# A 17-tap convolution by transforms of 48 tokens instead of 32, in groups of 16 graphs

## The chip, the core and the metric

The kernel runs on one core of a Trainium2 chip. A core has several engines that run side by side, each through its own list of instructions in order: TensorE (PE; its weight loads are listed as PEld) multiplies matrices into a memory of its own, PSUM; VectorE (DVE) and ScalarE (ACT) compute on PSUM and on the on-chip memory SBUF; GpSimd (POOL) computes on SBUF alone; SyncE (SP) issues transfers. Transfers between DRAM and SBUF can be issued by SyncE, ScalarE and GpSimd and are carried out by 16 DMA engines. The engines wait for each other through semaphores.

The metric is the time of one execution on the device, in microseconds (us). The kernel before took 2396.99 us (median of three runs, 2395.56 to 2398.62).

## What is computed

64 graphs of 256 tokens with 256 features, all in fp32, go through two layers. Layer 0 is a normalized graph convolution with a residual and a layer norm. Layer 1 takes its result `x` through two ways into a gated unit:

```python
xc = jnp.transpose(x, (0, 2, 1))
h = relu(bn1(conv1d(xc, conv1_w, 0)))            # 1 tap
h = bn2(conv1d(h, conv2_w, 8))                   # 17 taps, 256 -> 256 channels
x_conv = jnp.transpose(relu(h + xc), (0, 2, 1))
s = x @ w_se.T + b_se                            # 3 features
A = exp(-dist(s)) * adj
x_nmp = A @ relu(x @ w_msg.T + b_msg)
x_in = concat([x_conv, x_nmp], -1)
gi, gh = x_in @ w_ih.T + b_ih, x @ w_hh.T + b_hh # 3 * 256 outputs each
r, z = sigmoid(gi_r + gh_r), sigmoid(gi_z + gh_z)
y = (1 - z) * tanh(gi_n + r * gh_n) + z * x
out = layernorm(x + y)
```

The change concerns the second convolution, `conv2`, and the ways of data around it.

## The kernel before

`conv2` is done by the overlap-save method along the tokens. A window of `FL` = 32 tokens gives `NT` = 16 new outputs, because 17 taps need 16 more inputs. Each window is transformed to frequencies (a matmul with a fixed table), each frequency is multiplied by the transformed taps (a 256 x 256 matrix per frequency, again matmuls), and the inverse transform is done by additions and scaled additions on VectorE. A graph has `GT` = 256 / 16 = 16 windows, so that `Q` = 8 graphs fill the 128 partitions; there are `NQ` = 8 such groups.

The forward transform of a graph, a part of `layer1`:

```python
for k in range(DCH):                              # two halves of the channels
    p = bank("p_dft")
    for c, t0, t1 in ((0, 0, mid + 1), (1, mid - 1, GT)):
        first = t0 + 1 - c * mid
        nc.tensor.matmul(p[:, t0 * FL : t1 * FL], h[:, c, k * P : (k + 1) * P],
                         fwd[:, first : first + t1 - t0, :].rearrange("p t f -> p (t f)"), ...)
    nc.scalar.copy(V[:, :, k, g % Q * GT : (g % Q + 1) * GT], p.rearrange("p (t f) -> p f t", f=FL))
```

The products, two frequencies to a step. A complex frequency takes three real products, with `V` real, `V` imaginary and their sum `ab`; the taps `u` were transformed in a setup stage, stored in DRAM, and are loaded for each group again:

```python
def product(p, j, v, u):
    for k in range(DCH):
        nc.tensor.matmul(p[:, j * D : (j + 1) * D], v[:, k, :], u[:, k, :], start=k == 0, stop=k == DCH - 1)
# in products(), for each step:
for t, v in ((0, ab), (1, V[:, n0:n1]), (2, V[:, NF + n0 : NF + n1])):
    p = accbank(f"p_k{t}")
    for j in range(count):
        product(p, j, v[:, j], load_u(3 * (n0 + j) + t))
    p = half(p)[:, :count]
    if t == 0:   nc.scalar.copy(re, p)
    elif t == 1: nc.vector.tensor_add(im, re, p)
    else:        nc.vector.tensor_sub(re, re, p)
    yield
```

`FREQ` has 15 complex frequencies, and there are two real ones. The results go to a buffer `M` of their own. The inverse transform works in place in `M` (`even_frequencies`, `odd_frequencies`); the residual is added into `M` by a DMA that accumulates, issued by GpSimd; then `outputs` transposes `M` on TensorE and writes `xcT`, the gate's input with channels on the partitions, for the whole group:

```python
def residual(q, M):
    for i in range(4):
        nc.gpsimd.dma_start(M[:, i:16:4, :], xt[:, :, i % 2, i // 2, :], accum_op=ALU.add)
```

The gate of a graph, in two halves `c` of 128 tokens. Each half has two pieces on TensorE, `p_rz` and `p_n`:

```python
q = accbank("p_rz")                               # 6 matmuls of 512 columns
for j, (lhsT, w) in enumerate(hid + inp):
    nc.tensor.matmul(q, lhsT, w[:, : 2 * D], ...)
yield
p = accbank("p_n")                                # 6 matmuls of 256 columns
...
nc.vector.tensor_add(trz[:, c, :], q, brz_t)
nc.scalar.activation(trz[:, c, :], trz[:, c, :], AF.Tanh, scale=0.5)
...                                               # gn on VectorE, nn on ScalarE
# once per graph:
nc.gpsimd.tensor_tensor(total, x1, nn, op=ALU.add)
nc.gpsimd.tensor_tensor(x1, x1, nn, op=ALU.subtract)
...
layernorm(x1, nc.vector)
nc.sync.dma_start(out[g].rearrange("(c p) d -> p c d", p=P), x1)
```

Layer 0 and layer 1 of a graph leave `x1` (for the residual and the gate) and `xn` (for the gate) in DRAM; both stores are issued by GpSimd.

The stages are recorded piece by piece, so that pieces of several stages alternate in each engine's list; a scheduler may move instructions within it. A group's products alternate with gates of the group before, the inverse transform with further gates, and the graphs of the next group with the remaining pieces:

```python
for step in range(STEPS):                         # products of group q
    if step < 4: run(products(V, M, step))
    else:        run(merge(products(V, M, step), take(even, 2)))
    run(take(late, (0, 1, 1, 1, 2, 2, 2, 1)[step]))   # gates of the group before
run(even)
residual(q, M)
...                                               # late, odd and the first layer-0 pieces alternate
run(graphs(first, V, others))                     # layer 0 and 1 of the next 8 graphs, with early gates
```

Of the kernel before, what the change touches and what calls it, by code (L numbers as in the profile page):

```python
# [14 lines left out]
P = 128  # L15
# [11 lines left out]
def kernel(  # L27
# [36 lines left out]
    FL, NT = 32, 16  # L64
# [3 lines left out]
    assert N == 256 and D == 256 and B % Q == 0 and TAPS == FL - NT + 1  # L68
# [37 lines left out]
    make_identity(nc, ident)  # L106
    neg_half = const.tile([P, 4], F32)
# [61 lines left out]
    FREQ = (-8, 4, -12, 2, 10, -14, -6, 1, 5, 9, 13, -15, -11, -7, -3)  # L169
    NF = len(FREQ)  # L170
    NU = 3 * NF + 2
    SETS = (24, NU - 24)
    GC = 4
    GW = D // GC
    KT = GC * TAPS

    fm_rows = 2 * P + NT
    fm = dram.tile([fm_rows, FL], F32, name="fm")
    ud = [dram.tile([s * GC, GW, D], F32, name=f"ud{i}") for i, s in enumerate(SETS)]
    fwd = const.tile([P, GT // 2 + 2, FL], F32)  # L180
    dft_w = const.tile([KT, NU, GC], F32)

    def tables(pool):
        period = pool.tile([1, 512], F32, name="period")
# [3 lines left out]
        def wave(f, sine, n):  # L188

            first = 0 if not sine else (24 if f > 0 else 8)  # L190
            return period[:, first : first + abs(f) * (n - 1) + 1 : abs(f)]

        fwd_row = pool.tile([1, FL, FL], F32, name="fwd_row")
        w_row = pool.tile([1, TAPS, NU], F32, name="w_row")
        for n, f in enumerate(FREQ):
            nc.vector.tensor_copy(fwd_row[:, :, n], wave(f, False, FL))
            nc.vector.tensor_copy(fwd_row[:, :, NF + n], wave(-f, True, FL))

            c, d = wave(f, False, TAPS), wave(f, True, TAPS)
            nc.vector.tensor_copy(w_row[:, :, 3 * n], c)  # L200
            nc.vector.tensor_sub(w_row[:, :, 3 * n + 1], d, c)
            nc.vector.tensor_add(w_row[:, :, 3 * n + 2], c, d)
        for r in range(2):
            nc.vector.memset(fwd_row[:, :, 2 * NF + r], 1.0)
            nc.vector.memset(w_row[:, :, 3 * NF + r], 0.5)
        nc.vector.memset(fwd_row[:, 1::2, 2 * NF + 1], -1.0)
        nc.vector.memset(w_row[:, 1::2, 3 * NF + 1], -0.5)
# [5 lines left out]
        nc.gpsimd.dma_start(fm[P - 8 : P - 8 + FL].unsqueeze(0), fwd_row)  # L213
        for j in range(GT // 2 + 2):

            first = P - 8 + 8 - NT * (j - 1)
            nc.sync.dma_start(fwd[:, j, :], fm[first : first + P])


        wd = dram.tile([TAPS, NU], F32, name="wd")  # L220
        nc.gpsimd.dma_start(wd.unsqueeze(0), w_row)
        wt = pool.tile([KT, NU], F32, name="wt")
        for c in range(GC):
            nc.sync.dma_start(wt[c * NT : (c + 1) * NT], wd[:NT])
        nc.sync.dma_start(wt[GC * NT :], bcast_rows(wd[NT], NU, GC))
        mask = pool.tile([KT, GC], F32, name="mask")
        nc.vector.tensor_reduce(
            mask[: GC * NT], ident[: GC * NT, : GC * NT].rearrange("p (c t) -> p c t", c=GC), AX.X, ALU.add
        )
        nc.vector.tensor_copy(mask[GC * NT :], ident[GC * NT : KT, GC * NT : KT])  # L230
        nc.vector.tensor_mul(
            dft_w, wt.unsqueeze(2).to_broadcast([KT, NU, GC]), mask.unsqueeze(1).to_broadcast([KT, NU, GC])
        )

    def weights(pool, n, parts, scale):
# [5 lines left out]
        for c in range(GC):  # L241
            nc.sync.dma_start(tp[c * NT : (c + 1) * NT], taps[c, :NT])
        nc.sync.dma_start(tp[GC * NT :], taps[:, NT])
        nc.vector.tensor_mul(tp, tp, scale[:KT].unsqueeze(1).to_broadcast([KT, ng, D]))
        first = 0
        for i, count in enumerate(SETS):
            m = count * GC
            u = pool.tile([m, ng, D], F32, name=f"u_set{i}")
            for j in range(0, ng, 2):
                p = accbank("p_u").rearrange("p (g o) -> p g o", g=2)  # L250
                for h in range(2):
                    nc.tensor.matmul(  # L252
                        p[:m, h], dft_w[:, first : first + count, :].rearrange("p s c -> p (s c)"), tp[:, j + h],
                        start=True, stop=True,
                    )
                nc.scalar.copy(u[:, j : j + 2], p[:m])
            nc.gpsimd.dma_start(ud[i][:, n * ng : (n + 1) * ng], u)
            first += count
            yield
# [24 lines left out]

    x1_d = [dram.tile([Q, N, D], F32, name=f"x1_d{q}") for q in range(NQ)]
# [4 lines left out]
    def layer0(g):  # L290
# [5 lines left out]
        nc.vector.tensor_reduce(deg, a_t, AX.X, ALU.add)  # L296
# [51 lines left out]
        nc.gpsimd.dma_start(x1_d[g // Q][g % Q].rearrange("(c p) d -> p c d", p=P), x1)  # L348
        yield

    def layer1(g, V):

# [56 lines left out]
# [4 lines that stand above are left out]
# [7 lines left out]
                V[:, :, k, g % Q * GT : (g % Q + 1) * GT], p.rearrange("p (t f) -> p f t", f=FL)  # L420
# [20 lines left out]
        nc.gpsimd.dma_start(xn_d[g], xn)  # L441
# [4 lines left out]
    RE = (1, 4, 6, 8, 9, 10, 11) + tuple(range(16, 24))  # L446
    IM = (3, 5, 7, 12, 13, 14, 15) + tuple(range(24, 32))

    def load_u(slot):
        i, s = (0, slot) if slot < SETS[0] else (1, slot - SETS[0])  # L450
        u = ustream.tile([P, DCH, D], F32, name="u")
        nc.sync.dma_start(
            u, ud[i][s * GC : (s + 1) * GC].rearrange("c g o -> (c g) o").rearrange("(k p) o -> p k o", p=P)
        )
        return u
# [9 lines left out]
    def frequencies(step):  # L465
        return (0, 1) if step == 0 else (2 * step - 1, 2 * step + 1)

    AB = {}

    def sums(V, step):  # L470
        n0, n1 = frequencies(step)
        AB[step] = freq.tile([P, 2, DCH, P], F32, name="ab", bufs=2)
        nc.vector.tensor_add(AB[step][:, : n1 - n0], V[:, n0:n1], V[:, NF + n0 : NF + n1])

    def products(V, M, step):

        n0, n1 = frequencies(step)
        count = n1 - n0
        ab = AB.pop(step)
        if step + 1 < STEPS:  # L480
            sums(V, step + 1)
        if step == 0:
            p = accbank("p_real")
            for r in range(2):
                product(p, r, V[:, 2 * NF + r], load_u(3 * NF + r))
# [5 lines left out]
        def slots(of):  # L491
            by = of[n1 - 1] - of[n0] if count == 2 else 1
            return M[:, of[n0] : of[n0] + (count - 1) * by + 1 : by, :]

        re, im = slots(RE), slots(IM)
        for t, v in ((0, ab), (1, V[:, n0:n1]), (2, V[:, NF + n0 : NF + n1])):
            p = accbank(f"p_k{t}")
            for j in range(count):
                product(p, j, v[:, j], load_u(3 * (n0 + j) + t))
            p = half(p)[:, :count]  # L500
            if t == 0:
                nc.scalar.copy(re, p)
            elif t == 1:
                nc.vector.tensor_add(im, re, p)
            else:
                nc.vector.tensor_sub(re, re, p)
# [12 lines left out]
    def four(M, re, im):  # L519


        def parts(first, count):
            return bass.AP(
                tensor=M.tensor, offset=M.offset + first * D,
                ap=[list(M.ap[0]), [(im - re) * D, 2], [1, count * D]],
            )
        sub2(parts(re, 2), parts(re + 2, 2))
        sub2(parts(re, 1), parts(re + 1, 1))
# [3 lines left out]
    def turn(x, y, num, den):  # L532

        t = freq.tile([P, 2, D], F32, name="turn", bufs=2)
        a = math.pi * num / den
        stt = nc.vector.scalar_tensor_tensor
        if 2 * num <= den:
            tan = math.tan(a)
            stt(t[:, 0, :], y, -tan, x, op0=ALU.mult, op1=ALU.add)
            stt(t[:, 1, :], x, -tan, y, op0=ALU.mult, op1=ALU.subtract)  # L540
            return math.cos(a), t
        cot = 1.0 / math.tan(a)
        stt(t[:, 0, :], x, cot, y, op0=ALU.mult, op1=ALU.subtract)
        stt(t[:, 1, :], y, -cot, x, op0=ALU.mult, op1=ALU.subtract)
        return math.sin(a), t
# [4 lines left out]
    def even_frequencies(M):  # L550

        stt = nc.vector.scalar_tensor_tensor
# [12 lines left out]
        four(M, 8, 12)  # L565
# [3 lines left out]
        for i, num, x, y in ((1, 2, 9, 13), (2, 1, 10, 14), (3, 3, 15, 11)):  # L569
            by, t = turn(M[:, x, :], M[:, y, :], num, 8)  # L570
            stt(M[:, 8 + i : 16 : 4, :], t, -by, M[:, i:8:4, :], op0=ALU.mult, op1=ALU.add)
# [4 lines left out]
    def residual(q, M):  # L576

        xt = x1_d[q].rearrange("g (t a b c) d -> (g t) a b c d", t=GT, b=2, c=2)
        for i in range(4):
            nc.gpsimd.dma_start(M[:, i:16:4, :], xt[:, :, i % 2, i // 2, :], accum_op=ALU.add)  # L580

    def odd_frequencies(M):

        stt = nc.vector.scalar_tensor_tensor
        def parts(first, count, by=8):
            return bass.AP(
                tensor=M.tensor, offset=M.offset + first * D, ap=[list(M.ap[0]), [by * D, 2], [1, count * D]]
            )
        sub2(parts(16, 4), parts(20, 4))
        yield  # L590
        four(M, 16, 24)
        yield
        r = math.sqrt(0.5)
        add2(M[:, 20, :], M[:, 30, :])
        sub2(M[:, 28, :], M[:, 22, :])
        sub2(parts(21, 1), parts(23, 1))
# [267 lines left out]
```

## Time and profile before

| what | value |
|---|---|
| time, median of 3 | 2396.99 us |
| span of the profiled execution | 2394.0 us |
| busy: TensorE / VectorE / ScalarE / GpSimd | 2258.0 / 1422.7 / 712.9 / 546.0 us |
| DMA | 289.71 MB, mean 121 GB/s |
| loads of transformed taps (`u`) | 376 of 256 KB |
| granted TensorE clock, mean | 0.986 |

How to read the profile: "L460" is line 460 of the kernel. A group of instructions has its engine, its operation, the tile that it writes and those that it reads, the shape and the count. One fp32 matmul of the kernel appears as two records on PE; a transpose appears as one. In the table of stages each row is a stretch of the span with the busy time of each engine in it, the share of full speed at which TensorE's clock ran, and the share of the DMA engines' time with their GB/s. In the 40 slices a digit is a busy share in tenths.

### The profile page before, as it was taken

Reading aid. Unit: us, or ns where it says so; the run is one execution under the profiler, and the core shown is the slowest. Engines: PE = TensorE matmul, PEld = TensorE weight load, DVE = VectorE, ACT = ScalarE, POOL = GpSimd, SP = SyncE. Lnnn points to the kernel's source line nnn. Section 1 sums busy time; section 2 is a strip of 40 time slices with the busy share of each in tenths; the row PEclk is TensorE's granted clock in tenths of the full one; section 3 lists DMA queues with packets and bytes.
Section 4 is the critical chain, followed back from the end, with each engine's and each line's share of the span. In section 5 each row is a group of like instructions: output and inputs, shape, how many; then the busy total and the mean of one; then the engine's idle time right before and its main releaser. Section 6 shows DMA issues by size and latency. Waiting matters only on the chain.

```text
span 2394.0 us, 26937 instructions
## 1 busy us (share of the span) xinstructions
PE 2258.0 (94%) x9056; PEld 1604.4 (67%) x9056; DVE 1422.7 (59%) x3740; ACT 712.9 (30%) x1417; POOL 546.0 (23%) x587
## 2 busy tenths in 40 slices
PE   5999899999999999999999989999999999999997
PEld 4777666766777677766767666676677667776554
DVE  4445854776456845567456665477645684456644
ACT  2553253114331143212431134311433124321111
POOL 3220222213221222112220222221222122211122
PEclk8999999999999999999999999999999999999999
DMA  5777622743237322472225622274223732146121
GB/s 113 202 190 250 162 78 67 199 140 92 76 114 197 111 75 88 134 197 80 79 88 163 168 79 93 66 200 140 91 80 113 196 110 75 67 133 166 56 67 44
DMA packets 226018, 289.71 MB, mean 121 GB/s; under 512 B 19208, under 2 KB 202760, under 8 KB 224377
## 3 DMA queue, kind: packets, MB, share of 16 engines
q1 hardware_dynamic: 189112, 207.19, 29.3%
q0 software_dynamic: 33360, 79.88, 11.9%
q8 instruction: 72, 1.18, 0.2%
q10 hardware_dynamic: 3408, 0.93, 0.2%
q14 instruction: 66, 0.53, 0.1%
HBM read 208.46 MB, written 79.47 MB: 120 GB/s over the span
## 4 chain that ended last, share of the span: by engine, by line
PE 36%; issue 33%; POOL 12%; DVE 11%; DMA 5%; ACT 3%; SPq 0%; POOLq 0%; ACTq 0%; DVEq 0%
PE p_k L460 7%; PE p_rz L664 6%; PE p_n L669 5%; PE p_nmp L436 3%; PE p_dft L414 3%; POOL ln_rs L270 3%; DMA u<-ud 3%; POOL x_g L692 3%; POOL total L691 3%; PE p_u L252 2%; PE p_msg L392 2%; PE p_hT L330 2%; PE p_out L340 2%; DVE ln_st L267 1%; PE p_conv L368 1%
## 5 line engine op out<-in xcount | busy, mean ns | idle before, releaser
L664 PE MATMUL p_rz<-whh,xn_g 128*128 128x512 f32 x512 | 247.6, 600 | 0.0
L664 PE MATMUL p_rz<-wih,xcT 128*128 128x512 f32 x512 | 242.5, 594 | 4.8 <-ACT xcT L629 4.8
L664 PE MATMUL p_rz<-wih,xn_g 128*128 128x512 f32 x512 | 241.1, 593 | 0.0
L691 POOL TENSOR_TENSOR total<-x_g,nn 128x512 f32<-128x512 f32 x64 | 97.3, 1520 | 615.8 <-ACT nn L683 574.2
L460 PE MATMUL p_k<-u,V 128*128 128x256 f32 x960 | 222.7, 382 | 8.0 <-DMA u<-ud 7.0
L683 ACT ACTIVATE nn<-gn 128x256 f32<-128x256 f32 x128 | 53.3, 417 | 572.3 <-DVE gn L680 572.3
L460 PEld LDWEIGHTS p_k<-u,V 128*128 128x128 f32 x960 | 179.7, 190 | 41.7 <-issue 8.6
L674 ACT ACTIVATE trz<-trz 128x512 f32<-128x512 f32 x128 | 80.4, 628 | 416.8 <-DVE trz L673 297.6
L664 PEld LDWEIGHTS p_rz<-wih,xcT 128*128 128x128 f32 x512 | 96.5, 190 | 127.8 <-issue 117.5
L664 PEld LDWEIGHTS p_rz<-wih,xn_g 128*128 128x128 f32 x512 | 97.2, 191 | 120.4 <-issue 120.4
L673 DVE TENSOR_TENSOR trz<-p_rz,brz_t 128x512 f32<-128x512 f32 x128 | 87.2, 681 | 111.2 <-PE p_rz L664 111.2
L676 DVE TENSOR_TENSOR gn<-p_n,bn_t 128x512 f32<-128x512 f32 x128 | 88.1, 688 | 106.6 <-PE p_n L669 106.4
L270 POOL TENSOR_TENSOR ln_rs<-ln_rs,neg_half 128x2 f32<-128x2 f32 x128 | 95.9, 750 | 237.7 <-DVE ln_rs L269 164.2
L414 PE MATMUL p_dft<-fwd,h 128*128 128x288 f32 x512 | 140.2, 413 | 8.3 <-ACT h L373 3.6
L340 PE MATMUL p_out<-w,hT 128*128 128x256 f32 x512 | 129.0, 397 | 19.6 <-ACT hT L335 19.6
L392 PE MATMUL p_msg<-wmsg,xn 128*128 128x256 f32 x512 | 123.9, 385 | 21.4 <-DVE s L371 11.1
L280 ACT ACTIVATE x<-x,ln_mr,ln_rs 128x256 f32<-128x256 f32 x128 | 70.0, 593 | 242.5 <-DVE ln_mr L278 242.5
L669 PE MATMUL p_n<-whh,xn_g 128*128 128x256 f32 x512 | 138.4, 391 | 0.0
L431 DVE TENSOR_TENSOR aT<-aT,adjT 128x512 f32<-128x512 f32 x64 | 44.2, 691 | 154.0 <-ACT aT L430 154.0
L669 PE MATMUL p_n<-wih,xcT 128*128 128x256 f32 x512 | 133.3, 380 | 0.0
L664 PEld LDWEIGHTS p_rz<-whh,xn_g 128*128 128x128 f32 x512 | 94.3, 193 | 56.9 <-issue 51.7
L669 PE MATMUL p_n<-wih,xn_g 128*128 128x256 f32 x512 | 132.3, 381 | 0.0
(139 smaller groups left out, 4197.6 us busy)
## 6 DMA issues: line engine op xcount, KB each, us to landing
u<-ud SPq DMA_DIRECT2D x376, 256.0 KB, 3.8
xn_d<-xn POOLq DMA_DIRECT2D x64, 512.0 KB, 3.2
xn_g<-xn_d SPq DMA_DIRECT2D x64, 512.0 KB, 3.7
adj_t<-in_adj_dram SPq DMA_DIRECT2D x64, 256.0 KB, 3.0
x_t<-in_x_dram SPq DMA_DIRECT2D x64, 256.0 KB, 2.9
x_d<-x POOLq DMA_DIRECT2D x64, 256.0 KB, 3.2
x_g<-x_d SPq DMA_DIRECT2D x64, 256.0 KB, 2.7
M<-x_d POOLq DMA_DIRECT2D x32, 512.0 KB, 12.0
```

What stands on the lines that cost most here:

```text
L270: nc.gpsimd.tensor_tensor(rs, rs, neg_half[:, :NCH], op=ALU.pow)
L340: nc.tensor.matmul(p[:, c, :], hT[:, k, c * P : (c + 1) * P], w0[:, k, :], start=k == 0, stop=k == DCH - 1)
L392: nc.tensor.matmul(p[:, c, :], x1T[:, k, c * P : (c + 1) * P], wmsg[:, k, :], start=k == 0, stop=k == DCH - 1)
L414: nc.tensor.matmul(p[:, t0 * FL : t1 * FL], h[:, c, k * P : (k + 1) * P], fwd[:, first : first + t1 - t0, :].rearrange("p t f -> p (t f)") ...
L436: nc.tensor.matmul(p[:, k, :], msg[:, mc, k * P : (k + 1) * P], aT[:, mc].rearrange("p n q -> p (n q)"), start=mc == 0, stop=mc == NCH - 1,)
L460: nc.tensor.matmul(p[:, j * D : (j + 1) * D], v[:, k, :], u[:, k, :], start=k == 0, stop=k == DCH - 1)
L664: nc.tensor.matmul(q, lhsT, w[:, : 2 * D], start=j == 0, stop=j == len(terms) - 1)
L669: nc.tensor.matmul(p[:, o * D : (o + 1) * D], lhsT, w[:, 2 * D :], start=j == 0, stop=j == len(terms) - 1)
L673: nc.vector.tensor_add(trz[:, c, :], q, brz_t)
L674: nc.scalar.activation(trz[:, c, :], trz[:, c, :], AF.Tanh, scale=0.5)
L676: nc.vector.tensor_add(gn, p.rearrange("p (i d) -> p i d", i=2), bn_t)
L691: nc.gpsimd.tensor_tensor(total, x1, nn, op=ALU.add)
```

## The change

The window becomes `FL` = 48 tokens with `NT` = 32 new outputs, so that a graph has 8 windows and a group 16 graphs; there are 4 groups. A larger window spends a smaller part of its products on the 16 tokens that overlap. What goes with it:

- The products are written in place of their inputs: `V` and `M` are one buffer, `VM`. A second, half-size buffer `V2` takes the inputs of the first 8 graphs of the next group meanwhile, and ScalarE copies them over later.
- The taps are transformed with the real and the imaginary part; their sum and difference are made by GpSimd and VectorE. The setup stage covers 16 graphs.
- The inverse transform is rewritten (`real_transform`, `complex_begin` during the products, `complex_end` after them). Its outputs go to DRAM with tokens as rows (`xc_d`); each gate loads its graph's rows back, adds the residual by an accumulating DMA, and transposes them.
- The stores of `x1`, `xn` and `out` are issued by ScalarE; the degree sums and the last norm's scaling are done by ScalarE.

```diff
-    FL, NT = 32, 16
+    FL, NT = 48, 32
...
-    FREQ = (-8, 4, -12, 2, 10, -14, -6, 1, 5, 9, 13, -15, -11, -7, -3)
+    FREQ = tuple(3 * k for k in (-4, 2, -6, 1, 5, -7, -3)) + tuple(3 * k + 1 for k in (*range(8), *range(-8, 0)))
...
-        nc.vector.tensor_reduce(deg, a_t, AX.X, ALU.add)
+        for c in range(NCH):
+            nc.scalar.activation(unused, a_t[:, c, :], AF.Copy, accum_out=deg[:, c : c + 1])
...
-        nc.gpsimd.dma_start(x1_d[g // Q][g % Q].rearrange("(c p) d -> p c d", p=P), x1)
+        nc.scalar.dma_start(x1_d[g // Q][g % Q].rearrange("(c p) d -> p c d", p=P), x1)
...
-        nc.gpsimd.dma_start(xn_d[g], xn)
+        nc.scalar.dma_start(xn_d[g], xn)
...
+    VM = freq.tile([P, FL, D], F32, name="VM")
+    V, M = VM.rearrange("p f (k q) -> p f k q", k=DCH), VM
...
+        for t, v in ((1, of_pair(V, RE, step)), (0, ab), (2, of_pair(V, IM, step))):
+            q = accbank(f"p_k{t}")
+            for j, n in enumerate(PAIRS[step]):
+                product(q, j, v[:, j], load_u(n, t))
+            p[t] = half(q)[:, :count]
+            if t == 0:
+                nc.scalar.copy(re, p[0])
+            elif t == 2:
+                nc.vector.tensor_add(im, re, p[1])
+                nc.vector.tensor_sub(re, re, p[2])
+            yield
...
+    def output(q, n, re, im):
+        plain = M[:, n // 8 * 8 + ORDER.index(n % 8), :]
...
+        for j in range(2):
+            stt(M[:, low + 16 * j, :], t[:, j, :], by[j], plain, op0=ALU.mult, op1=ALU.add)
+        nc.gpsimd.dma_start(
+            xc_d[q].rearrange("g (t a b) d -> (g t) a b d", a=2, b=16)[:, :, n, :], M[:, low : low + 17 : 16, :]
+        )
...
+        xc = gate.tile([P, NCH, D], F32, name="xc_g")
+        nc.sync.dma_start(xc, xc_d[g // Q][g % Q].rearrange("(c p) d -> p c d", p=P))
...
+    def residual(g):
+        nc.gpsimd.dma_start(
+            GATE[g][2], x1_d[g // Q][g % Q].rearrange("(c p) d -> p c d", p=P), accum_op=ALU.add
+        )
...
+    def transposed(g):
+        x1, xn, xc = GATE[g]
+        xcT = gate.tile([P, DCH, N], F32, name="xcT")
+        p = bank("p_xcT").rearrange("p (k n) -> p k n", k=DCH)
         for k in range(DCH):
+            for c in range(NCH):
+                nc.tensor.transpose(p[:, k, c * P : (c + 1) * P], xc[:, c, k * P : (k + 1) * P], ident)
+            nc.scalar.activation(xcT[:, k], p[:, k], AF.Relu, bias=bn2[:, 1, k : k + 1])
+        GATE[g] = x1, xn, xcT
...
-        layernorm(x1, nc.vector)
-        nc.sync.dma_start(out[g].rearrange("(c p) d -> p c d", p=P), x1)
+                layernorm(x1, nc.scalar)
+                nc.scalar.dma_start(out[g].rearrange("(c p) d -> p c d", p=P), x1)
...
+    AHEAD = Q // 2
+    V2 = ahead.tile([P, FL, DCH, AHEAD * GT], F32, name="V2")
...
             else:
-                run(merge(products(V, M, step), take(even, 2)))
-            run(take(late, (0, 1, 1, 1, 2, 2, 2, 1)[step]))
-        run(even)
-        residual(q, M)
+                run(merge(products(step), take(real, 1)))
+                run(complex_begin(step))
+            if q:
+                run(take(late, (0, 1, 1, 1, 1, 1, 2, 1, 2, 1, 2, 1)[step]))
+            else:
+                run(take(begin, 2 + step // 4))
+        run(real)
+        if not q:
+            run(merge(begin, end, 3))
+        elif more:
+            run(merge(merge(take(late, 18), take(begin, 6), 3), take(end, 8), 3))
+            run(begin)
+        else:
+            run(merge(late, end, 2))
         if more:
...
+            run(late)
+            run(end)
+            for f in range(0, FL, 12):
+                nc.scalar.copy(V[:, f : f + 12, :, : AHEAD * GT], V2[:, f : f + 12])
+            early = gates(q, range(EARLY))
+            others = [take(early, 2) for _ in range(Q)]
+            run(graphs(first, range(AHEAD, Q), V, others))
+            run(early)
+            late = gates(q, range(EARLY, Q))
         else:
-            run(outputs(M, xcT))
-            run(gates(q, range(Q), xcT))
+            run(gates(q, range(Q)))
```

## The prediction

> **What bounds the kernel now.** I read the busy shares first, then two stretches of TensorE's timeline for its pace, then the busy table of chosen stages, then the groups that the change touches.
>
> The page's busy shares and slices:
>
> ```profile
> PE 2258.0 (94%) x9056; PEld 1604.4 (67%) x9056; DVE 1422.7 (59%) x3740; ACT 712.9 (30%) x1417; POOL 546.0 (23%) x587
> PE   5999899999999999999999989999999999999997
> ```
>
> TensorE is busy nearly everywhere; no other engine exceeds 59%. Busy time alone does not say how near TensorE is to its rate, because matmuls overlap. The timeline of TensorE in the last gate stage does (start, busy, group):
>
> ```profile
> 2280.81 1.88 PE L664 MATMUL p_rz<-whh,xn_g 128*128 128x512 f32 x4
> 2282.53 1.88 PE L664 MATMUL p_rz<-wih,xn_g 128*128 128x512 f32 x4
> 2284.25 1.88 PE L664 MATMUL p_rz<-wih,xcT 128*128 128x512 f32 x4
> 2285.96 1.03 PE L669 MATMUL p_n<-whh,xn_g 128*128 128x256 f32 x4
> ```
>
> Four records of 512 columns start 1.72 us apart: 430 ns each. Four of 256 columns, in the same timeline, take 0.865 us: 216 ns each. So 0.84 ns a column, against listed durations of 600 and 382 ns. I use these paces (also 242 ns for 288 columns, 109 ns for 128).
>
> At these paces the work of TensorE is: 1536 records of 512 columns, 660 us; 5856 of about 256 (1536 p_n, 1504 p_k and p_real, 2560 in five other groups, 256 p_u), 1265; 512 p_dft, 124; 256 p_dist, 45 by the page; 896 of 128, 98. Sum 2192 us of 2394. **Only 202 us are lost**, so this is a TensorE-bound kernel, and what removes columns from it removes time.
>
> Where the 202 lie, by stage (window, us, PE, PEld, DVE, ACT, POOL busy, clock, DMA share, GB/s):
>
> ```profile
> 60.00:200.00 140.00, 134.24 (x631) 102.98 (x630) 59.95 (x173) 80.51 (x158) 35.06 (x47) 1.00 0.70 192
> 420.00:480.00 60.00, 59.60 (x232) 43.73 (x231) 44.80 (x84) 7.28 (x14) 12.86 (x11) 1.00 0.73 204
> 780.00:840.00 60.00, 54.30 (x201) 36.68 (x200) 52.31 (x132) 13.15 (x26) 13.94 (x13) 0.97 0.35 102
> 1140.00:1200.00 60.00, 59.23 (x270) 44.20 (x269) 28.24 (x86) 27.74 (x56) 15.70 (x18) 1.00 0.27 84
> 2280.00:2340.00 60.00, 60.00 (x185) 34.91 (x184) 28.07 (x65) 8.37 (x16) 12.92 (x12) 1.00 0.23 70
> ```
>
> Products (420) and pure gates (2280) run at the pace. Comparing starts with paces, the turn after the products (780), where VectorE runs the inverse transform, loses about 12 us with its surroundings; graph stages (1140) lose 2 to 4 us per 40 us; the first 200 us lose about 50 and the end 13. Eight turns at 12 make about half of the loss.
>
> **What the Trainium skill says.** "Perfetto Trace Analysis", Identifying the Most-Contended Engine: matmul busy share is no good measure of nearness to the roofline. The trace agrees: 382 ns listed, 216 ns of pace. "TensorE: Matmul & The Clock Gate", Back-to-back issue gap, gives 518 cycles for 512 columns, an estimated 216 ns at its 2.4 GHz; these fp32 records take 430, so I take the trace. Its section Why this matters for your kernels warns that idle gaps lower the clock: 0.97 at the turn, 1.00 around it. "DMA: Bandwidth & Descriptors", Issuing engines are not separate DMA queues: moving a transfer to another engine saves issuing time only. No run yet shows the move; I credit it with nothing beyond GpSimd's issue time.
>
> **The change part by part.**
>
> *Products.* Tokens per transform go from 32 (16 new) to 48 (32 new), groups from 8 graphs to 16. Before, 15 frequencies at 3 products plus 2 real ones, two chunks each, 8 groups: 752 matmuls = 1504 records. After, 23 at 3 plus 2: 71 x 2 x 4 = 568 = 1136 records. Saved 368 x 0.216 = **79.5 us** on the path.
>
> *Forward transform.* p_dft goes from 288 to 240 columns: 512 x 48 x 0.84 ns = **20.6 us** saved. All other counts on TensorE stay, the 256 transposes too, only with another source. TensorE's work becomes 2192 - 100 = 2092 us.
>
> *VectorE.* The convolution's sums, combinations and inverse transform now cost 535 us (the rows with M, ab or turn). Counting the changed kernel's instructions at 0.42 us per 256, 0.69 per 512, 1.22 per 1024, 2.29 per 2048 columns gives 506. The degree sum (42.7) and the output norm's last step (47.1) move to ScalarE; a tail of 128 small operations replaces 64 (+10); tables and weights add about 28. Sum 1423 - 29 - 43 - 47 + 10 + 28 = 1342 us. None of it is on the path except at the turns.
>
> *ScalarE.* Added: 128 degree passes at 0.51 (65 us), 128 norm passes at 0.59 (76), copies from the second input buffer, 12 of 1536 columns at about 1.5 us (18); smaller evictions cancel the rest: about 860 us. It also issues 192 stores, 0.4 us each by its issues at the start (77 us). In all some 40% of the span, beside TensorE.
>
> *GpSimd.* Issues cost 150 us before (48.9 + 36.8 + 55.1 + 8.9). After, 64 output stores and 64 accumulating loads at about 0.76 us (97), 48 table stores (27), 16 additions of 1024 columns at 2.9 (46): 170. No change.
>
> *Transfers.* 92 fewer loads of u (-24.1 MB), the convolution's output out and back (+33.5 MB): 290 to about 299 MB, at a mean of 130 GB/s against 251 in the busiest slice.
>
> *The order.* In the changed program the residual's accumulating load stands three graphs ahead of the gate that needs it, and the first gate group after the last convolution has about 8 half-graph gate pieces (62 us of TensorE) in front. So the way through DRAM (M<-x_d took 12 us) should be hidden, also in the last stage.
>
> *Losses after.* Turns: 4 instead of 8. VectorE needs about 79 us at its pace for the end of a transform and the nine gate halves placed with it, TensorE about 75: nearly level, so 7 us lost in each of three. In the first there are no gates yet, only graphs: 74 us of VectorE against some 60 of TensorE, so 15 to 20 us lost. Together about 40 with the restart of layer 0, against 96. Setup now covers 16 graphs: +12; the weight transform stands ahead of the first graph's conv1 and waits for a scale that went through DRAM (bn_scale issued at 37.3 us in the trace), +6. The 48 graphs beside gates or products lose as before. Stores in ScalarE's in-order queue wait for earlier transfers to free their semaphores and hold up evictions: +15, a guess. The product stage carries the inverse transform's first half, VectorE about 80 us per 114: +5. Net 202 - 56 + 12 + 6 + 15 + 5 = 184; because I trust these losses less than the work, I take 195.
>
> 2092 + 195 = 2287 us of span, and 3 more in the timing: **2290 us**.
>
> **Rivals.** (1) *VectorE becomes the bound at the turn and in the products.* It shows 52.3 of 60 us busy at 780. For: larger groups bring the work in larger lumps, and in-place products forbid the next group's input before the last output is stored. Against: half of the next group's input has a buffer of its own, and the order spreads the lumps over gates. It would cost 10 to 20 us per turn: 2330 to 2350. (2) *ScalarE's queue.* Each store must wait for its data and a free semaphore while TensorE's evictions stand behind it. For: in graph stages ScalarE is busy 27.7 to 34.5 us in 60 already. Against: a store's data come from ScalarE itself, so they are nearly ready. At 0.5 us of TensorE's time per store: +96 us, 2370 or more. (3) *The way through DRAM is not hidden in the last 16 gates*: a wait of 5 us each makes +80. (4) *Fewer turns save more than I grant*: losses of 160 give 2255.
>
> **Range and chances.** The 100 us of TensorE are counted, not guessed; losses can be 155 to 260. That gives 2245 to 2350. The 2% line is 2349, which only rival 2 or 3, or several waits together, reach. Faster by over 2%: 0.87; within 2%: 0.08; slower: 0.05.
>
> **What would show it.** p_k and p_real at 1136 records, p_dft at 240 columns, pace still 216 ns: else the sum is wrong. ScalarE at 850 to 870 us busy, VectorE at about 1340. TensorE's waits: few on DMA for xc_g, some on VectorE at three or four turns. If ScalarE leads TensorE's waits in graph stages, rival 2 is right; if the last 250 us show gaps per graph, rival 3; if VectorE shows nine tenths around the turns with TensorE below eight, rival 1.

## The result, and the profile after

The changed kernel takes 2340.34 us (median of four runs, 2333.61 to 2345.6), against 2396.27 us of the kernel before on the same chip. The ratio is 0.9767, with a 95% interval of 0.9738 to 0.9797. The prediction was 2290 us, in a range of 2245 to 2350: the direction and the range held, and half of the expected gain of 107 us did not come. Where that half went is the question of what follows.

The page's busy shares and TensorE's slices, after:

```profile
PE 2176.7 (93%) x8688; PEld 1540.5 (66%) x8688; DVE 1366.0 (58%) x3733; ACT 845.0 (36%) x1857; POOL 595.7 (25%) x603
...
PE   4999999988999988999999998899999999999997
```

TensorE has 368 records fewer (9056 to 8688), and there is still no other engine above 58%. New are the eights in the slices: slices 9 and 10, 15 and 16, 25 and 26 of 40, which lie at the first three turns after a group's products.

TensorE's timeline among the products (start, busy, group) gives the paces:

```profile
731.71 1.88 PE L729 MATMUL p_rz<-wih,xcT 128*128 128x512 f32 x4
733.42 1.89 PE L469 MATMUL p_k<-u,VM 128*128 128x256 f32 x8
735.15 1.89 PE L469 MATMUL p_k<-u,ab 128*128 128x256 f32 x8
736.88 1.89 PE L469 MATMUL p_k<-u,VM 128*128 128x256 f32 x8
```

Four records of 512 columns take 1.71 us, eight of 256 take 1.73: the paces of before. The 512 records of p_dft now follow each other at 203 ns. The work at these paces is 2091 us, as the prediction had it (2092). The span of the profiled run is 2343.8, so **253 us are lost, where 203 were lost before and 195 were predicted**. The error is in the losses alone.

I split both runs at two kinds of borders that can be read from TensorE's records, the first p_real and the last p_k of each group. In each part the work is its records times the paces, and the rest is loss:

| part | before: us, of them lost | after: us, of them lost |
|---|---|---|
| setup, up to the first products | 209.5, 50.1 | 325.2, 71.1 |
| products, all groups | 590.3, 14.3 | 443.5, 8.2 |
| from the first group's products to the second's | 170.6, 26.7 | 259.0, 40.0 |
| turns, gates and graphs between the later products | 1233.8 in six, 91.1 | 895.9 in two, 106.3 |
| after the last products | 189.8, 20.8 | 420.1, 27.3 |
| sum | 2394.0, 203.0 | 2343.8, 252.9 |

Busy times in four of the parts after (window, us; PE, PEld, DVE, ACT, POOL busy; clock, DMA share, GB/s):

```profile
0.00:325.20 325.20, 281.81 (x1281) 221.47 (x1281) 161.40 (x614) 170.58 (x397) 120.50 (x145) 0.97 0.53 159
...
421.80:680.80 259.00, 235.38 (x1008) 172.10 (x1007) 164.30 (x491) 120.72 (x272) 63.17 (x67) 0.98 0.33 109
680.80:796.10 115.30, 114.27 (x452) 84.36 (x452) 82.25 (x159) 19.67 (x38) 19.75 (x16) 1.00 0.68 204
796.10:1242.80 446.70, 412.09 (x1658) 288.75 (x1658) 247.14 (x725) 182.87 (x412) 111.86 (x113) 0.98 0.33 103
```

In the last line VectorE is busy 55% of the time and ScalarE 41%, and TensorE loses 52 us. Such means hide short stretches in which an engine is full; the part on the prediction comes back to that. Here I looked at the waits first. TensorE's chief ones, after (waiter, what it waits for: us in all, times, longest):

```profile
PE p_msg L400 <- DVE s L379: 39.9, 34, 6.9
PE p_xcT L707 <- ACT xcT L708: 35.0, 14, 6.3
PE p_rows L409 <- DVE scols L392: 13.5, 12, 2.0
...
PE p_k L469 <- DMA u<-ud: 5.1, 6, 1.0
```

Before, the first of these was 11.1 us in 6 times. It is not a wait for data: p_msg needs x1T and weights, both long there. It needs a PSUM bank of the pool of three, and the oldest holds conv1's result until VectorE has read it (L379, L380). The longest such waits lie at the turns. One of them, in the timelines of GpSimd, VectorE and TensorE:

```profile
897.13 1.24 POOL L696 DMA_DIRECT2D xc_g<-x_d  x1 [1.83 <-DMA xn_g<-xn_d]
897.92 1.75 POOL L756 TENSOR_TENSOR total<-x_g,nn 128x512 f32<-128x512 f32 x1
899.75 1.27 POOL L757 TENSOR_TENSOR x_g<-x_g,nn 128x512 f32<-128x512 f32 x1
...
901.05 1.74 DVE L758 SCALAR_TENSOR_TENSOR x_g<-trz,x_g 128x512 f32<-128x512 f32 x1 [3.86 <-POOL x_g L757]
...
903.45 0.60 PE L318 MATMUL p_adjT<-ident,adj_t 128*128 128x128 f32 x4
...
907.70 0.15 DVE L379 TENSOR_TENSOR s<-p_conv,bse 128x3 f32<-128x3 f32 x1
...
908.33 2.96 PE L400 MATMUL p_msg<-wmsg,xn 128*128 128x256 f32 x8 [4.28 <-DVE s L379]
```

It reads upwards. TensorE stands 4.28 us until VectorE reads conv1. VectorE got there late because a gate's step, ahead of it in its own queue, stood 3.86 us for GpSimd's difference. GpSimd was late in part by its own two sums (1.75 and 1.27 us) and in part because its queue had stood before the accumulating transfer that adds the residual: ScalarE had nn ready at 896.35 (start 895.93, 0.42 us), the first sum starts at 897.92. Three in-order queues pass a delay on to an engine that needed none of these results.

### The profile page after: what moved, and what is told of

It is laid out like the page before. It is cut to its first block, busy times and chain, and to the rows that moved or that the text cites. A ratio compares the mean times of both kernels' runs of the same rounds, so it can differ in the third digit from the quotient of the medians.

```text
span 2343.8 us, 26631 instructions
## 1 busy us (share of the span) xinstructions
PE 2176.7 (93%) x8688; PEld 1540.5 (66%) x8688; DVE 1366.0 (58%) x3733; ACT 845.0 (36%) x1857; POOL 595.7 (25%) x603
## 4 chain that ended last, share of the span: by engine, by line
PE 50%; DVE 17%; issue 14%; POOL 10%; DMA 6%; ACT 3%; SPq 0%; ACTq 0%; POOLq 0%; DVEq 0%
PE p_rz L729 18%; PE p_n L738 8%; PE p_k L469 8%; DMA xc_g<-xc_d 3%; PE p_nmp L445 3%; PE p_dft L422 3%; PE p_msg L400 2%; PE p_hT L338 2%; POOL ln_rs L276 2%; PE p_out L348 2%; POOL total L756 2%; DVE ln_st L273 2%; POOL x_g L757 2%; POOL u_set L261 2%; DVE x L352 1%
## 5 line engine op out<-in xcount | busy, mean ns | idle before, releaser
L696 POOL DMA_DIRECT2D xc_g<-x_d x64 | 78.7, 1236 | 525.1 <-DMA xc_g<-xc_d 381.3
L400 PE MATMUL p_msg<-wmsg,xn 128*128 128x256 f32 x512 | 131.4, 402 | 49.5 <-DVE s L379 39.9
L469 PE MATMUL p_k<-u,VM 128*128 128x256 f32 x736 | 175.0, 380 | 1.6 <-DMA u<-ud 1.6
L469 PEld LDWEIGHTS p_k<-u,VM 128*128 128x128 f32 x736 | 138.9, 190 | 29.7 <-issue 8.2
L758 DVE SCALAR_TENSOR_TENSOR x_g<-trz,x_g 128x512 f32<-128x512 f32 x64 | 53.7, 839 | 170.7 <-POOL x_g L757 169.5
L338 PE MATMUL p_hT<-adjT,x 128*128 128x256 f32 x512 | 126.9, 393 | 19.6 <-DVE adjT L321 11.7
L400 PEld LDWEIGHTS p_msg<-wmsg,xn 128*128 128x128 f32 x512 | 96.5, 197 | 72.0 <-issue 40.1
L331 POOL TENSOR_TENSOR x_t<-x_t,b_t 128x512 f32<-128x512 f32 x64 | 83.0, 1298 | 238.5 <-ACT x L330 199.4
L307 POOL TENSOR_TENSOR dis<-deg,neg_half 128x2 f32<-128x2 f32 x64 | 47.0, 735 | 366.8 <-DVE deg L305 352.8
```

Source lines behind the costliest of these rows:

```text
L331: nc.gpsimd.tensor_tensor(x_t, x_t, b0_t.unsqueeze(1).to_broadcast([P, NCH, D]), op=ALU.add)
L338: nc.tensor.matmul(p[:, k, :], x1[:, mc, k * P : (k + 1) * P], adjT[:, mc, 1 - mc : 3 - mc, :].rearrange("p n q -> p (n q)"), start=mc == ...
L400: nc.tensor.matmul(p[:, c, :], x1T[:, k, c * P : (c + 1) * P], wmsg[:, k, :], start=k == 0, stop=k == DCH - 1)
L696: nc.gpsimd.dma_start(GATE[g][2], x1_d[g // Q][g % Q].rearrange("(c p) d -> p c d", p=P), accum_op=ALU.add)
```

## Experiments

Each is the changed kernel with the edit named; the ratio is to the kernel before.

| kernel | us | ratio, 95% interval |
|---|---|---|
| the change | 2340.3 | 0.9767 [0.9738, 0.9797] |
| degree on VectorE again | 2342.5 | 0.9786 [0.9765, 0.9807] |
| convolution loaded first | 2346.7 | 0.9795 [0.9776, 0.9815] |
| transposes ahead of both relus | 2325.1 | 0.9711 [0.9693, 0.9728] |
| stores off ScalarE's queue | 2364.2 | 0.9876 [0.9856, 0.9897] |
| no residual (left out) | 2313.0 | 0.9663 [0.9649, 0.9678] |
| norm's product on GpSimd | 2334.4 | 0.9754 [0.9739, 0.9770] |
| banks 4 and 4 | 2344.4 | 0.9797 [0.9763, 0.9831] |
| no arithmetic in the transform's second half (left out) | 2287.7 | 0.9558 [0.9538, 0.9577] |
| residual summed in DRAM | 2334.9 | 0.9749 [0.9735, 0.9764] |
| four edits | 2314.0 | 0.9662 [0.9646, 0.9678] |
| three edits | 2309.4 | 0.9643 [0.9629, 0.9658] |
| five edits | 2320.2 | 0.9704 [0.9684, 0.9723] |

And the losses of the profiled runs in the same parts, in us (gates 1 and 2 are the two stretches between later products):

| kernel | setup | products | first turn | gates 1 | gates 2 | end | sum |
|---|---|---|---|---|---|---|---|
| the change | 71.1 | 8.2 | 40.0 | 51.9 | 54.4 | 27.3 | 253 |
| transposes first | 73.8 | 8.9 | 39.2 | 47.3 | 45.7 | 21.5 | 236 |
| stores off ScalarE | 78.5 | 9.1 | 44.2 | 55.3 | 56.4 | 26.2 | 270 |
| no residual | 68.3 | 3.4 | 39.4 | 40.7 | 39.8 | 25.9 | 218 |
| no arithmetic | 66.1 | 8.9 | 33.5 | 36.0 | 30.9 | 14.8 | 190 |
| residual in DRAM | 77.8 | 4.4 | 46.1 | 44.9 | 42.3 | 26.3 | 242 |
| three edits | 65.3 | 7.8 | 36.0 | 39.3 | 38.1 | 27.8 | 214 |
| five edits | 65.0 | 8.6 | 37.2 | 45.7 | 40.7 | 26.5 | 224 |

### The degree back on VectorE

```diff
-        for c in range(NCH):
-            nc.scalar.activation(unused, a_t[:, c, :], AF.Copy, accum_out=deg[:, c : c + 1])
+        nc.vector.tensor_reduce(deg, a_t, AX.X, ALU.add)
```

> One part undone: the degree is a row sum on VectorE again. Theory A (VectorE's in-order queue, which waits 85 us for the degree on ScalarE, arrives late at the banks of conv1 and lets TensorE stand before p_msg): that wait goes to 0, VectorE's busy time grows from 1366 by 64 sums of about 0.6 us to about 1404 us, TensorE's stalls between p_adjT and p_msg fall from 53 to about 35 us, time 2322 us (2315 to 2330). Theories B (GpSimd's queue held by the residual transfers), C (stores on ScalarE) and the transposes of p_xcT: 2340 within 5. If VectorE's amount of work is what binds in the turns: 2345 to 2350.

Measured: 2342.5 us, no difference clear of the noise. VectorE's wait of 85 us for the degree is gone, its busy time is 1410 us, and TensorE's wait of p_msg for L379 is 37.5 us (39.9 before the edit). Theory A is out for the change as it stands: a long wait in a list need not delay what matters.

### The convolution loaded first

```diff
     def load_gate(g):
+        xc = gate.tile([P, NCH, D], F32, name="xc_g")
+        nc.sync.dma_start(xc, xc_d[g // Q][g % Q]...)
         x1 = gate.tile([P, NCH, D], F32, name="x1_g")
         ...                                  # x1 and xn as before, xc no longer after them
```

> One order changed: of the three loads for a graph's gates the convolution (xc_g) goes first, ahead of x1_g, whose buffer waits for an output store. Theory B (GpSimd stands 381 us before the accumulating residual transfer, and the layer norms and the gates' sums stand behind it): the wait before L696 falls below 200 us, VectorE's wait for the difference on GpSimd falls from 169 to about 110 us, time 2322 us (2315 to 2330). Theories A, C: 2340 within 5.

Measured: 2346.7 us, no gain. GpSimd's wait for the convolution fell from 381 to 305 us, but 55 us of it came back as a wait for TensorE in front of the same instruction. The edit did not do what it was for, so it says little about theory B; the residual needed a stronger one.

### Transposes ahead of both relus

```diff
         for k in range(DCH):
             for c in range(NCH):
                 nc.tensor.transpose(p[:, k, c * P : (c + 1) * P], xc[:, c, k * P : (k + 1) * P], ident)
+        for k in range(DCH):
             nc.scalar.activation(xcT[:, k], p[:, k], AF.Relu, bias=bn2[:, 1, k : k + 1])
```

> One order changed: the four transposes of p_xcT go ahead of both relus, where now the second two wait for the first relu, which stands on ScalarE behind a tanh that waits for VectorE. Theory D (this coupling costs TensorE directly): the wait of p_xcT for ScalarE falls from 35 us to about 0 and time to 2310 us (2305 to 2318). If the stall only moves on to the next wait on the same late VectorE: 2330 to 2340.

Measured: 2325.1 us, 15 less. The wait of p_xcT for ScalarE (35.0 us) is gone from the list, and a part of it turns up one use later, at the gates' matmuls that take xcT:

```profile
PE p_rz L730 <- ACT xcT L709: 14.8, 5, 5.5
```

Both expectations are half right: the order costs TensorE directly, and 15 of the 35 us were only moved on.

### Stores off ScalarE's queue

```diff
-        nc.scalar.dma_start(x1_d...)      # and xn_d
+        nc.gpsimd.dma_start(x1_d...)      # and xn_d
-                nc.scalar.dma_start(out[g]...)
+                nc.sync.dma_start(out[g]...)
```

> One part undone: the 192 stores of x1, xn and the output leave ScalarE's queue, for GpSimd's (128) and SyncE's (64), as before the change. Theory C (the prediction's 15 us for stores that hold up ScalarE's evictions): 2325 us (2318 to 2332), with ScalarE's results on time. Theory B: GpSimd's in-order queue gets 128 more issues of 0.7 us and is held more often, 2350 to 2365 us. Theory A alone: 2340 within 5.

Measured: 2364.2 us, 24 *more*. This is what theory B expected (2350 to 2365). The prediction's +15 for these stores had the wrong sign: of the two placements tried, ScalarE's queue is the cheaper. On GpSimd a store stands until ScalarE has written its data, and GpSimd's sums and powers stand behind it:

```profile
POOL xn_d L450 <- ACT xn L449: 245.8, 36, 14.1
```

TensorE's waits for VectorE grew by 7 us before p_msg and 8 before p_rows (to 47.2 and 21.1). VectorE's wait for GpSimd's difference did not grow (152.4 us against 169.5), so the way by which the delay reaches TensorE is not shown, and the three stores were not moved one at a time.

### The residual left out

The 64 accumulating transfers that add x1 to the convolution are left out, so this kernel computes less.

```diff
     def residual(g):
-        nc.gpsimd.dma_start(GATE[g][2], x1_d[g // Q][g % Q]..., accum_op=ALU.add)
+        return
```

> Leaves work out: the 64 accumulating transfers that add x1 to the convolution ahead of the transposes. Theory B at its limit (GpSimd's queue held 381 + 109 us in front of them): if GpSimd's waiting reaches TensorE, 2320 us or less; after the changed order of loads, which took 76 us from the DMA part of that wait and gave 55 us to its other part and nothing to the time, rather 2335 to 2345. VectorE's wait for the difference on GpSimd (169 us) should fall by 60 us or more either way.

Measured: 2313.0 us, 27 less. The two stretches of gates lose 11 and 15 us less, the setup and the first turn hardly anything. VectorE's wait for GpSimd's difference falls less than expected, from 169.5 to 133.6 us, but its longest from 5.8 to 3.2; and p_msg's longest wait falls from 6.9 to 2.5 us. So theory B holds in kind, and the long holds are what shrank most; but this edit takes the transfers away together with the waiting.

### The norm's product on GpSimd

```diff
+            nc.vector.tensor_scalar(mr, mv[:, :, 0], -1.0, None, op0=ALU.mult)
         nc.gpsimd.tensor_tensor(rs, rs, neg_half[:, :NCH], op=ALU.pow)
...
-            nc.vector.scalar_tensor_tensor(mr, mv[:, :, 0], -1.0, rs, op0=ALU.mult, op1=ALU.mult)
+            nc.gpsimd.tensor_tensor(mr, mr, rs, op=ALU.mult)
```

> One operation moved: the product of mean and 1/sigma of the layer norms, at which VectorE's queue waits 112 us for GpSimd's power, is computed on GpSimd, right after the power (VectorE only turns the mean's sign, before it). Theory A2 (short waits in VectorE's queue, this one above all, are what brings it late to conv1's banks): the wait of 112 us goes, stalls between p_adjT and p_msg from 53 to about 30 us, time 2318 us (2310 to 2328). Rival (the queue is late by the work in it, not by this wait, as the degree's 85 us were worth nothing): 2340 within 5. Each norm comes about 0.6 us later on ScalarE, which may cost up to 5 us.

Measured: 2334.4 us, 6 less, with intervals that overlap. VectorE's wait of 112 us is gone and it reaches conv1 in time, but TensorE then stands elsewhere:

```profile
PE p_xcT L709 <- ACT xcT L710: 46.7, 12, 6.7
PE p_dft L424 <- ACT h L383: 21.3, 24, 1.6
...
PE p_msg L402 <- DVE s L381: 10.5, 14, 1.8
```

### One bank more for the graphs

```diff
-    ps = ... bufs=3      psacc = ... bufs=5
+    ps = ... bufs=4      psacc = ... bufs=4
```

> One size changed: the graphs' pool of PSUM banks gets 4 instead of 3, the products' and gates' pool 4 instead of 5. Theory E (p_msg stands because the banks of conv1 are still held when VectorE comes late, whatever makes it late): the stall between p_adjT and p_msg falls from 53 us to 15 or less, that before p_rows may take over some of it, time 2305 us (2295 to 2318). Rival 1 (the stall moves to the next use of what VectorE delivers late): 2330 to 2340. Rival 2 (the accumulators' pool lacks the bank): stalls at p_k and p_rz, 2345 or more.

Measured: 2344.4 us, no difference clear of the noise. The waits of p_msg for conv1's banks are gone, and the 33 us appear at the next thing that needs VectorE, whose data p_rows needs:

```profile
PE p_rows L409 <- DVE scols L392: 46.6, 32, 2.9
PE p_xcT L707 <- ACT xcT L708: 34.9, 15, 6.3
```

By the waits rival 1 is right, though the time lies above its range. The bank was where the delay showed, not what made it.

### The transform's second half without its arithmetic

All VectorE arithmetic of `complex_end` is left out; the stores write what lies in the buffer. The order of the rest is kept.

```diff
     def output(q, n, re, im):
-        t = freq.tile(...); by = [real_part(t[:, j, :], x, y, ...) for j in range(2)]
-        for j in range(2):
-            stt(M[:, low + 16 * j, :], t[:, j, :], by[j], plain, op0=ALU.mult, op1=ALU.add)
         nc.gpsimd.dma_start(xc_d[q]..., M[:, low : low + 17 : 16, :])
     # complex_end: four, add2, sub2, turned and four_turned go likewise
```

> Leaves work out: all of VectorE's arithmetic in the second half of the inverse transform (some 60 us of VectorE per group of 16 graphs); its stores stay, of what lies in the buffer. Theory F (the turns, some 38 + 25 + 25 + 14 us of loss where the prediction had 40 in all, are lost to VectorE's arithmetic there): time falls to 2270 us (2255 to 2285), with almost no loss left in the three later turns. Rival (the turns lose through order and buffers, and the arithmetic lies beside the gates): 2310 to 2335.

Measured: 2287.7 us, 53 less, between the two expectations. VectorE does 185 us less (1181 against 1366 us busy). The loss falls by 6.5 at the first turn, 16 and 23.5 in the stretches of gates and 12.5 at the end. Looking closer at the first of those stretches, the turn itself (796 to 920 us in the change) loses 24 us and its graphs beside gates 28; without the arithmetic the corresponding pieces lose 6 and 30. So the arithmetic makes the turn's loss and not the graphs'. Over the 120 us of that turn VectorE is busy only 95 us, but in 840 to 860 us it is busy 92% of the time and TensorE 69%; in these 20 us lies TensorE's longest wait of the turn:

```profile
800.00:920.00 120.00, 103.36 (x350) 65.67 (x349) 95.05 (x248) 31.86 (x72) 41.65 (x42) 0.94 0.41 121
840.00:860.00 20.00, 13.73 (x42) 8.93 (x41) 18.35 (x43) 4.21 (x9) 6.66 (x7) 0.83 0.41 118
...
849.24 0.69 PE L707 MATMUL p_xcT<-ident,xc_g 128*128 128x128 f32 x2 [6.26 <-ACT xcT L708]
```

### The residual summed in DRAM

To separate GpSimd's queue from the mere leaving out: the whole result is computed, with no transfer for the residual in GpSimd's queue.

```diff
         nc.scalar.dma_start(x1_d[g // Q][g % Q]..., x1)
+        nc.scalar.dma_start(xc_d[g // Q][g % Q]..., x1)
...
-        nc.gpsimd.dma_start(xc_d[q]..., M[:, low : low + 17 : 16, :])
+        nc.gpsimd.dma_start(xc_d[q]..., M[:, low : low + 17 : 16, :], accum_op=ALU.add)
```

> The residual is added at another place, with the whole result computed: layer0 stores x1 a second time, into the convolution's place in DRAM (64 more issues on ScalarE of about 0.4 us), and the 64 stores of the convolution accumulate there (issues on GpSimd 1.2 instead of 0.7 us), so that the 64 transfers with their waits in front of GpSimd's sums fall away. If those waits, and not the bytes moved, made the 27 us that leaving the residual out gained: 2318 us (2310 to 2326). If it was the transfers themselves, which remain in number and bytes: 2335 to 2345. Should accumulating into DRAM be slow or come late for the last gates, more than 2345.

Measured: 2334.9 us, only 6 less and within the noise, which by the total alone would blame the transfers themselves. The table of parts says otherwise: the stretches of gates lose 7 and 12 us less, much of what leaving it out gained, and the products 4 less. The setup loses 7 more and the first turn 6 more. For the first turn the trace shows a single event. SyncE issues the graphs' input loads behind the gates' loads, and xc_g now waits for the accumulating stores:

```profile
520.31 0.93 SPq L692 DMA_DIRECT2D xc_g<-xc_d  x2
521.35 0.41 SPq L93 DMA_DIRECT2D adj_t<-in_adj_dram  x1
...
526.51 0.42 ACT L304 ACTIVATE unused<-adj_t 128x256 f32<-128x256 f32 x1 [4.93 <-DMA adj_t<-in_adj_dram]
...
527.44 1.22 PE L439 MATMUL p_dist<-dist_r,dist_l 32*128 32x256 f32 x2 [3.18 <-ACT V L428]
```

The adjacency matrix comes late, ScalarE's queue stands 4.93 us for it, and TensorE 3.18 us behind ScalarE. The setup takes 331.9 us here, where setups of unchanged code lie between 320.2 and 327.9 us. In it TensorE now waits 8.7 us for ScalarE before p_dft, which it did for 0.3 us in the change. The run with four edits below, which has the same extra stores on ScalarE, has 335.7 us of setup and 22.7 us of such waits; with three edits, without these stores, it is 319.4 and 10.2. So the extra stores in ScalarE's queue have a cost there.

### Edits together

Four together: the residual in DRAM, transposes first, the norm's product on GpSimd, 4 and 4 banks.

> Four edits together: residual accumulated in DRAM, transposes ahead of both relus, the norm's product on GpSimd, 4 and 4 banks. If the late arrivals sit one behind the other (each alone only moves the stall to the next use: conv1's banks, p_rows, p_dft, p_xcT), removing them together gains more than the sum of the single ones (about 20 + 15 + 6 + 0): 2285 us (2275 to 2298). If they add up: 2299 us. If VectorE's work is the common limit: 2305 to 2318.

The same without the residual in DRAM:

> The same without the changed residual: transposes ahead of both relus, the norm's product on GpSimd, 4 and 4 banks. Sum of the single ones 2319 us; with the stalls' common chain broken 2300 to 2312; if the stall before p_rows and p_dft stays as it is with 4 banks, 2322 to 2330.

Measured: 2314.0 and 2309.4 us. **The three edits gain 31 us, where singly they gave 15 + 6 - 4**, of which only the 15 is clear of the noise. This fits delays that pass from one queue to the next and are worth something once the places to which they moved are open as well; but the surplus of 14 us is no larger than the uncertainty of the four differences together, and no pair of the edits was run. The fourth edit adds nothing. At 2309.4 us this version beats both kernels, by 3.6% and 1.3%. TensorE's chief waits in it (28 us at most, against 40) are:

```profile
PE p_dft L424 <- ACT h L383: 28.3, 35, 1.4
PE p_rz L732 <- ACT xcT L711: 23.0, 8, 6.3
PE p_rows L411 <- DVE scols L394: 20.8, 15, 3.4
```

Last, the three edits with two more: the degree on VectorE, and there also the sum of the weights' transform (`nc.gpsimd.tensor_tensor(us[2]...)` becomes `nc.vector.tensor_add(us[2]...)`).

> The three edits of the run before (transposes ahead of both relus, the norm's product on GpSimd, 4 and 4 banks; 2309 us) with two more: the degree on VectorE again, which alone changed nothing, and the sum of the weights' transform on VectorE ahead of its difference, instead of on GpSimd (56 us of waiting of VectorE in the setup). If a wait of VectorE costs nothing by itself, as the degree's did alone: 2309 within 5, with the setup no shorter than 319 us. If these waits counted and were only covered by the ones now removed: 2295 us (2288 to 2302), the setup 310 us or less. VectorE's busy time grows by some 55 us; should work bind rather than waiting, 2315 to 2325, lost in the stages with gates.

Measured: 2320.2 us, 11 more. The setup is as long as before (319.1 us), so VectorE's wait of 56 us there cost nothing. VectorE is busy 1416 us instead of 1350, and the profiled run loses its 9 us in the stretches of gates, as the third reading expected. So moving the degree to ScalarE, a part of the change, is worth something here, where other waits are out of the way: in the change itself undoing it cost nothing that shows.

## Why the prediction was right where it was, and where it failed

- **TensorE's work.** 1136 records of products, 240 columns in p_dft, paces unchanged: 2091 us against 2092. The counted 100 us came in full.
- **Busy times.** ScalarE 845 us (predicted 850 to 870), VectorE 1366 (1342), both near. GpSimd's issues for stores, residual and tables were put at 170 us with the additions; by the rows they are 44.8 + 78.7 + 26.4 + 37.5 = 187, because an accumulating issue takes 1.24 us, not 0.76. Transfers 305 MB instead of 299.
- **Way through DRAM hidden.** Right: in the last 290 us TensorE runs at its pace up to its last matmul, 13 us before the end, and xc_g is not in TensorE's waits on transfers. Rival 3 is out. But the hidden way has a cost elsewhere: its residual transfer holds GpSimd's queue, which the prediction had not counted, for it looked at GpSimd's issue times only.
- **Products +5.** The loss went from 14.3 to 8.2, 6 less.
- **Setup +18** (12 + 6). Right: +21. The wait before the first p_u for the scaled taps is 7.4 us.
- **Stores on ScalarE +15, a guess; rival 2.** Wrong in sign: undoing it makes the kernel 24 us slower.
- **"Turns: 4 instead of 8 ... together about 40 ... against 96".** This is the step that failed, in its overlap and not in its amounts. "VectorE 79 about against TensorE 75: nearly level, so 7": the end of the transform and the nine gate halves do lie in 796.5 to 890 us, with VectorE busy 79.3 us and TensorE's work at its pace 78.4. But they took 93.5 us, so that 15 are lost, and the 30 us behind them lose 9 more, with the stall of 4.28 us shown above that hangs on GpSimd. Two level loads did not overlap fully. The kernel before loses 9 us in its turn (784 to 870 us), nearly all in the first 56, where VectorE is as full:

```profile
784.30:840.00 55.70, 50.00 (x181) 32.90 (x180) 49.06 (x122) 12.05 (x24) 13.24 (x12) 0.97 0.34 99
796.50:890.00 93.50, 81.83 (x271) 49.78 (x269) 79.26 (x200) 22.50 (x50) 32.37 (x33) 0.96 0.41 121
```

That is 0.15 and 0.16 us lost per us of this lump of VectorE's work (8.5 in 55.7, 15.1 in 93.5): the lump grew with the group, and its loss with it. In the first turn, for which the prediction had 15 to 20, the lump (422 to 500 us) loses 12.5, and 27 are lost behind it, for which it had nothing.

- **"The 48 graphs beside gates or products lose as before".** Also wrong, by less. Before they lose 2.1 us per 40 us (870 to 990 us), after 3.5 (920 to 1243 us). Leaving the residual out brings it back to 2.8, the three edits to 2.6.

The sum of it: the prediction lowered the losses by 56 for turns and raised them by 38 for the rest. Measured, setup +21, products -6, and everything with turns and graphs +35 instead of -41 (-56 + 15): 203 becomes 253. That the time stayed in the range rests on the counted work and on a wide range for the losses (155 to 260, which by the prediction's own sum give 2250 to 2355 and not 2245 to 2350).

Rival 1 came nearest: by its number (2330 to 2350), by place, and in good part by its reason. Its sign, nine tenths on VectorE with TensorE below eight, is not in the page's slices, which are 58.6 us wide (VectorE reaches 8 at most); in narrower windows it is: 92% and 69% in 840 to 860 us. In the first turn VectorE is 97% busy for 60 us:

```profile
440.00:500.00 60.00, 52.78 (x233) 38.45 (x232) 58.10 (x175) 26.78 (x65) 18.39 (x22) 1.00 0.34 128
```

Leaving the arithmetic out takes 18 of the 24 us of the first later turn. The three edits, which leave nearly all of its amount (1350 us busy in all, against 1366), take 5. So most of that loss needs VectorE's lump, and a smaller part comes from the order.

Open: what the first turn's 40 us consist of beyond the 6.5 of arithmetic. Of the 27 us behind its lump (500 to 681 us) 24 stay when the arithmetic is left out; TensorE's listed waits there add up to 15 us, mostly for VectorE, none over 2.5. Of the edits that keep all work, none took more than 5 of the 40.

## What to carry to other kernels

When a change makes larger lumps of the same work, fewer of them need not cost less: here the loss grew with the length of the lump. Ask what stands behind the lump in each in-order queue, and price the turn by that; level sums of busy time do not say that the two overlap. Look for a full engine in windows shorter than the lump. A wait in the list names the place where a delay surfaces; a bank or a wait removed there moves it to the next place, so test the source, and judge edits together as well as singly. Ask of each transfer what its issuing queue must wait for, and which computing stands behind it: stores were cheaper here in the queue of the engine that makes their data.

## What was unexpected of the hardware

The size of one thing: after a stall of some microseconds TensorE runs at half its pace for a while. After 6.94 us of waiting the eight records of p_msg take 3.54 us from their start to the next group's, where eight take 1.73:

```profile
1472.17 3.74 PE L400 MATMUL p_msg<-wmsg,xn 128*128 128x256 f32 x8 [6.94 <-DVE s L379]
1475.71 0.41 PE L409 MATMUL p_rows<-ident,scols 128*128 128x128 f32 x2
```

The Trainium skill, "TensorE: Matmul & The Clock Gate", Why this matters for your kernels, warns of it for gaps above about 3 us, and the trace agrees: of the eleven stalls above 3 us after TensorE's first matmul in the change, ten are followed, in the 8 us after them, by 1.4 us or more beyond the pace. In all, 163 records of the change (p_dist, whose starts are uneven at any time, left out) follow at about half pace, which makes 33 us of the 253 (129 records and 25 us before). All but two of the 163 start within 8 us after a stall above 1 us. So this stall of 7 us costs 9, and many stalls below 1 us cost less than few long ones of the same sum.

An accumulating transfer of 256 KB costs GpSimd 1.24 us to issue (78.7 us for 64), a plain one 0.70 (44.8 for 64).
